# Kept turned blocks for the first SAGE pass of a two-layer graph network, its sixteen slots in a new order, two of six tests a graph in the gated part

## The chip, the cores and the metric

The kernel runs on one core of a Trainium2 chip, as one program. The metric is the device time of one execution in microseconds. Engines are named as the profile names them: PE is the matrix engine (PEld its weight loads), DVE the vector engine, ACT the scalar engine, POOL the GpSimd engine, and SP the engine that issues most DMAs here. Each engine runs its instructions in the order in which the program lists them, and waits on semaphores that other engines and landed DMAs raise.

## The reference, cut to what matters

There are 16 graphs of 1024 nodes and 128 channels, with a 0/1 adjacency. Layer 0 is a gated graph network of four steps on all graphs; layer 1 first thins the adjacency by a "skipping" that goes row by row, and then runs three SAGE layers with batch norm. Both layers are added to their input and normalised.

```python
def _gru_cell(m, h, ...):                       # layer 0, four times for each graph
    r, z, n = sigmoid(..), sigmoid(..), tanh(xn + r * hn)
    return (1.0 - z) * n + z * h

def step(carry, n):                             # layer 1: the skipping, row after row
    row = jnp.take(carry, n, axis=0)
    num, rank = jnp.sum(row), jnp.cumsum(row)
    sf = jnp.where(num > T_DIL, (num + K_DIL - 1) // K_DIL, 1)
    rm = row & (rank % sf == 0)
    carry = carry.at[n].set(row & ~rm)                 # removed from the row
    carry = carry.at[:, n].set(carry[:, n] & ~rm)      # and from the column

def _sage(x, adj, Wr, Wx, b, mf):               # three times, batch norm between
    deg = jnp.clip(jnp.sum(adj, axis=-1, keepdims=True), 1.0, None)
    out = (jnp.einsum('bij,bjd->bid', adj, x) / deg) @ Wr + x @ Wx + b
    return out / jnp.maximum(jnp.linalg.norm(out, axis=-1, keepdims=True), 1e-12) * mf[..., None]
```

## The kernel before, in words

The order of every engine's instructions is written out by hand: the program text is the order, and pools of rotating tiles decide only which buffer a tile gets, and with it what a refill has to wait for.

**The gated part** (classes `Gated` and `FixPoint`) takes the first 1280 us. Two graphs run through the four steps of layer 0 in turn (streams 0 and 1, `layer`), and between PE's matmuls `beside` puts the steps of the skipping, one piece at each of ten points `aside(0)` to `aside(9)` of a layer. The skipping works on blocks of 128 rows of four graphs at once. For block row k of a graph it needs what earlier block rows removed from its first k*128 columns: these are read back from DRAM (`not_r`), turned by a transposing DMA into a tile `f_rt` (`read_back`, `read_last`), and `keep` (L729) applies them. The signed result of each block row, which has -0.5 or 0.5 at an edge and 0 elsewhere, goes to `not_r` in DRAM in bf16 (`rows`, L867). Each pair of layers also tests one block of 128 rows of the adjacency for values other than 0 and 1 (`load_test`, `check`, `look` at L1982); two of the eight blocks of a graph are tested here.

**The first SAGE pass** (`Sage.first`) takes the next 470 us. The loop runs over b from -1 to 15, and each turn has sixteen slots, t = 0 to 15 (`slot`). A slot holds work on graph b (`now`) and work that prepares graph n = b + 1 (`nxt`):

- For graph n, sixteen *units* build the thinned adjacency turned, `p_at`, an fp32r tile. A unit turns four blocks of `not_r` on PE (p_u, L1482). Where a block lies above the diagonal, ACT makes it 0 or 1 with a Relu (L1487). Elsewhere DVE compares the block of `p_nr` in place with the turned block in PSUM (L1495, `unit_low`). POOL then *packs* each half row to bytes (`pack`, L1503, tile p_b), which go to DRAM in two halves for the later passes (L1689 and L1681, `s_at`).
- Graph n's input is normalised (L1517 to L1531), turned (L1418) and split into two parts, p_xh by ACT (L1412) and p_xl by POOL (L1413).
- For graph b, PE aggregates with 8 + 8 matmuls of 512 columns for each half (`agg`, L1564, p_xh then p_xl). ACT evicts each half to s_ag (`evict`, L1570; two buffers), writes the degree row in f16 (L1551), PE turns it to columns (L1557), DVE makes 1/degree from it (L1559, L1560). PE multiplies with the weights (`out_first`, L1579 to L1584), DVE scales (L1388, L1389), ACT squares (L1396, L1397), DVE makes the rows s_r (L1402 to L1407), and these are split again into p_rh (ACT) and p_rl (POOL).
- PE aggregates a second time with p_rh and p_rl, for the next SAGE layer. ACT evicts these two banks to s_ag at slot 15, and SP writes them to DRAM at slot 1 of the next turn (L1702).
- DVE tests the remaining six blocks of a graph, which SP loads (p_a, L1458, L1982).

The loop's work for graph 0 also holds `first_weights` (L1304 to L1310), which needs weights that `load_given` loads in the turn b = -1. `constants` stands ahead of the loop.

After it come the second and third pass and the head, which the change does not touch.

Of the kernel before, what the change touches and what calls it, by code (L numbers as in the profile page):

```python
# [21 lines left out]
P = 128  # L22
# [607 lines left out]

class FixPoint:
# [20 lines left out]
    def __init__(self, ctx, tc, cst, adj, not_r, bad):  # L652
        self.tc, self.nc, self.cst, self.adj, self.not_r, self.bad = tc, tc.nc, cst, adj, not_r, bad
        nc, G = self.nc, self.G
# [69 lines left out]

    def keep(self, i, g, a):
        k = self.todo[i][0]
        if k:
            rt = self.left.pop((i, g))
            self.nc.vector.scalar_tensor_tensor(a[:, :k * P], rt[:, :k * P], 0.0, a[:, :k * P],  # L729
                                                op0=ALU.is_ge, op1=ALU.mult)  # L730
# [9 lines left out]
    def steps(self):  # L740
# [5 lines left out]
        for i, (k, b0) in enumerate(self.todo):  # L746
# [41 lines left out]
            self.count(i, 1, a[1], rank, pt)  # L788
            if i == 0:

                for c in range(G, self.LOTS):
                    self.load(c)
# [125 lines left out]
class Gated:  # L918
# [72 lines left out]
    def load_test(self, n):  # L991
        if n < B * 2:
            self.test = self.wk.tile([P, N], F32, name="h_test", bufs=1)
            self.nc.sync.dma_start(self.test, self.adj[n // 2, n % 2 * P:(n % 2 + 1) * P, :])

    def check(self, n):
        junk = self.wk.tile([P, N], BF, name="h_junk", bufs=1)
        look(self.nc, junk, self.bad, self.test, n // 2, n % 2)
# [160 lines left out]
    def beside(self, st, ot, l, s, b0, steps):  # L1159
# [33 lines left out]
        def aside(n):  # L1193
# [8 lines left out]
            if n == 1 and s == 1 and not checked:  # L1202
                self.check(b0 // 2 * L0 + l)
                checked.append(l)
# [5 lines left out]
class Sage:  # L1210
# [14 lines left out]
    def __init__(self, ctx, tc, cst, adj, not_r, summed, nodemask, W, vec, Wl, bl, out, bad):  # L1225
        self.tc, self.nc, self.cst = tc, tc.nc, cst
# [29 lines left out]
    def load_given(self):  # L1256
# [10 lines left out]
        nc.sync.dma_start(self.vr[9:, :], row(bl))  # L1267
        self.m48 = self.wk.tile([P, NB, C], F32, name="p_rh", bufs=1).rearrange("p a b -> p (a b)")[:3 * B, :]
# [31 lines left out]
    def first_weights(self):  # L1300
# [9 lines left out]
        nc.vector.tensor_copy(self.mask48, self.m48)  # L1310
# [111 lines left out]
    def first(self):  # L1422

        nc, tc, cst = self.nc, self.tc, self.cst
        with ExitStack() as c:
# [17 lines left out]
            self.load_s(0)  # L1443
            self.eps = self.const([P, 1], 1e-5, "s_eps")
# [5 lines left out]
            self.constants()  # L1450
# [10 lines left out]
    def load_nr(self, b, f):  # L1461
        if b < B:
            g = self.g.setdefault(b, {})
            if f == 0:
                g["nr"] = self.nrp[b % 2].tile([P, NB, N], BF, name="p_nr")
            self.nc.sync.dma_start(g["nr"][:, 4 * f:4 * f + 4, :], rows_of(self.not_r[b, f * HF:(f + 1) * HF, :]))
# [7 lines left out]
    def unit(self, b, t):  # L1474

        nc, g, f, j = self.nc, self.g[b], t // 8, t % 8
        if t == 0:
            g["at"] = self.atp[b % 2].tile([P, NB, N], FR, name="p_at")
        v, at = g["nr"], g["at"]
        pu = self.ps2.tile([P, HF], F32, name="p_u")  # L1480
        for i in range(4):
            nc.tensor.matmul(pu[:, i * P:(i + 1) * P], v[:, 4 * f + i, j * P:(j + 1) * P], self.cst["ident_b"],  # L1482
                             start=True, stop=True)
        low = min(max(j + 1 - 4 * f, 0), 4) * P
        c0 = f * HF
        if low < HF:
            nc.scalar.activation(at[:, j, c0 + low:c0 + HF], pu[:, low:], AF.Relu, scale=2.0)  # L1487
        g["pu"] = pu, low

    def unit_low(self, b, t):  # L1490

        g, f, j = self.g[b], t // 8, t % 8
        (pu, low), c0, v = g.pop("pu"), f * HF, g["nr"]
        if low:
            self.nc.vector.scalar_tensor_tensor(g["at"][:, j, c0:c0 + low], v[:, j, c0:c0 + low], 0.0, pu[:, :low],  # L1495
                                                op0=ALU.is_lt, op1=ALU.is_lt)

    def pack(self, b, t):
# [4 lines left out]
        self.nc.gpsimd.tensor_copy(g["b", f][:, j, :], g["at"][:, j, f * HF:(f + 1) * HF].bitcast(F32))  # L1503
# [38 lines left out]
    def degrees(self, b, f):  # L1542
# [7 lines left out]
        nc.vector.tensor_scalar(g["rho"][:, cols], deg, 1.0, None, op0=ALU.min)  # L1550
        nc.scalar.copy(g["row"][:, cols], deg)  # L1551

# [9 lines left out]
    def agg(self, pa, hi, at, f, js, start, stop):  # L1562
        for n, j in enumerate(js):
            self.nc.tensor.matmul(pa, hi[:, j, :], at[:, j, f * HF:(f + 1) * HF],  # L1564
# [37 lines left out]

    def slot(self, b, t):

        nc, g, n = self.nc, self.g.get(b), b + 1
        now, nxt = b >= 0, n < B

        if nxt:
# [4 lines left out]
            if t in (10, 13):  # L1613
                self.load_a(n, 2 + t // 13)
        if now and t in (0, 2, 5, 8):
            self.load_a(b, (0, 2, 5, 8).index(t) + 4)

        if now:
            if t in (2, 5):
                g["ag", t // 5] = self.evict(g.pop(("pa", t // 5)), -1, 0)  # L1620
            if t == 15:
                g["ag2"] = [self.evict(g.pop(("pb", f)), b, f) for f in range(2)]
        if nxt:
            self.unit(n, t)
            if t != 6 or not now:
                self.unit_low(n, t)
            if t:
                self.pack(n, t - 1)
        if now and t == 0:
            self.pack(b, 15)  # L1630
        if now:
            bank = lambda: self.ps3.tile([C, HF], F32, name="p_ag")
            if t in (2, 5):
                self.degrees(b, t // 5)
            if t in (0, 1, 3, 4):
# [4 lines left out]
            if t in (5, 7):  # L1640
                self.out_first(b, t // 7)
            if t in (6, 8):
                f = t // 8
                g["o", f] = self.scale_rows(b, f, g.pop(("oa", f)), g.pop(("ob", f)))
                if t == 6 and nxt:
                    self.unit_low(n, t)
# [3 lines left out]
            if t in (7, 9):  # L1650
                f = t // 9
                g["r", f] = self.rows(b, f, g.pop(("o", f)), g.pop(("ss", f)))
            if t in (8, 10):
                self.split_r(b, t // 10)
            if t in (6, 8):
                g["ss", t // 8] = self.squares(g["o", t // 8])
            if t in (11, 13):
                self.turn_r(0, b, t // 13, self.ps1)
            if t in (9, 10, 12, 14):
                part = g["rl"] if t in (10, 14) else g["rh"]  # L1660
                js = range(4 * (t // 12), 4 * (t // 12) + 4)
                for f in range(2):
                    if t == 9:
                        g["pb", f] = bank()
                    self.agg(g["pb", f], part, g["at"], f, js, t == 9, t == 14)

        if nxt:
# [4 lines left out]
            if t in (6, 8):  # L1672
                self.turn_x(n, t // 8)
            if t in (7, 12):
                self.split_x(n, t // 12)
        if now and t in (2, 5, 8, 10, 12, 14):
            self.check(b, (2, 5, 8, 10, 12, 14).index(t) + 2)

        if now:
            if t == 2:  # L1680
# [4 lines left out]
            if t in (13, 15):  # L1685
                nc.sync.dma_start(self.rt[b, t // 15], g["rt", t // 15])
        if nxt:
            if t == 10:
                nc.sync.dma_start(self.at8[n, 0], self.g[n]["b", 0])  # L1689
            if t == 13:  # L1690
                nc.sync.dma_start(self.x1[n], self.g[n]["s"])
        if (b, t) == (-1, 11):
            self.load_given()
# [4 lines left out]
        if (b, t) == (0, 3):  # L1698
            self.first_weights()
# [316 lines left out]
def kernel(ctx: ExitStack, tc: tile.TileContext, x, adj, nodemask,  # L2016
# [7 lines left out]
    with ExitStack() as ctx:  # L2024
        dram = ctx.enter_context(tc.tile_pool(name="e_dram", bufs=1, space=DRAM))
        not_r = dram.tile([B, N, N], BF, name="e_nr")
        summed = [dram.tile([P, NB, C], F32, name=f"e_sum{b}") for b in range(B)]
        with ExitStack() as c:
            gru = Gated(c, tc, cst, x, adj, weight, w_ih, w_hh, b_ih, b_hh, summed, bad)
            fix = FixPoint(c, tc, cst, adj, not_r, bad)  # L2030
            c.enter_context(tc.manual_schedule(engines={ET.PE, ET.DVE, ET.Activation, ET.Pool, ET.SP}))
            gru.run(fix.steps())
        sage = Sage(ctx, tc, cst, adj, not_r, summed, nodemask, W, vec, Wl, bl, out, bad)
# [34 lines left out]
```

## Time and profile before

| what | time |
|---|---|
| median of 3 runs | 2207.2 us (2204.59 to 2207.37) |
| the profiled execution | 2207.94 us |
| its span, first to last instruction | 2206.2 us |
| PE busy | 2099.8 us, 95% |
| DVE busy | 1836.0 us, 83% |
| ACT busy | 1327.2 us, 60% |
| POOL busy | 1233.9 us, 56% |
| mean granted TensorE clock | 0.986 |

The profile's lines are read like this. A group of instructions has its line in the kernel, engine, operation, out<-in, and how often it ran; then busy time and mean duration; then how long the engine sat idle just before them, and who ended that. A row of the order of time gives start, duration, engine, line, operation, tiles, and in brackets the idle time before it with its releaser. A row of a stretch gives, for each engine, busy time and number of instructions, then the granted clock, the busy share of the 16 DMA engines and GB/s. A row of waits says who waited for whom, in total, how many times, and the longest.

### The profile page before, as it was taken

What the parts mean: (1) busy time and instruction counts of PE and PEld (TensorE: products, weight loads), DVE (VectorE), ACT (ScalarE), POOL (GpSimd) and SP (SyncE); (2) the same over time, 40 slices, a digit from 0 to 9 for tenths busy, and PEclk for the clock granted to TensorE, in tenths of its full rate; (3) what the DMA queues carried; (4) which work ended last, traced back from release to release, by engine and by line L of the source; (5) the groups of instructions that cost most, each with busy time, mean ns of one, the idle gap of its engine ahead of it and who ended that gap; (6) DMA issues with size and microseconds to landing.
All of it is one profiled execution on the core that took longest, in us unless ns stands there. A gap on an engine that the chain in (4) does not pass through costs nothing. (4 is left out here: it accounts for less than half of the span.)

```text
span 2206.2 us, 32924 instructions
## 1 busy us (share of the span) xinstructions
PE 2099.8 (95%) x10217; PEld 1441.5 (65%) x10217; DVE 1836.0 (83%) x4213; ACT 1327.2 (60%) x3238; POOL 1233.9 (56%) x1218
## 2 busy tenths in 40 slices
PE   6999999999999999999999979999999899999987
PEld 4666556666666665666655657777777678887865
DVE  4898998889998889989889978888888666766877
ACT  3657466565656666465575656666666355555756
POOL 4458558567476475585575457777777255540002
PEclk9999999999999999999999989999999999999989
DMA  8247446366364394472584178888887577764404
GB/s 254 76 107 244 90 115 223 85 179 184 84 202 129 80 256 110 91 241 78 126 237 101 52 263 309 304 306 306 305 305 259 210 249 248 248 225 171 139 30 143
DMA packets 233853, 406.13 MB, mean 184 GB/s; under 512 B 79042, under 2 KB 100196, under 8 KB 233668
## 3 DMA queue, kind: packets, MB, share of 16 engines
q1 hardware_dynamic: 187844, 284.37, 39.4%
q0 software_dynamic: 41472, 117.46, 19.8%
q10 hardware_dynamic: 4352, 2.11, 0.4%
q8 instruction: 83, 1.36, 0.2%
q14 instruction: 102, 0.84, 0.1%
HBM read 313.48 MB, written 109.25 MB: 192 GB/s over the span
## 5 line engine op out<-in xcount | busy, mean ns | idle before, releaser
L1104 PE MATMUL h_g<-h_h,h_wh 128*128 128x512 f32 x768 | 396.1, 597 | 3.3 <-DVE h_r L1116 3.3
L1104 PE MATMUL h_g<-h_ms,h_wi 128*128 128x512 f32 x768 | 392.2, 592 | 0.0
L1123 POOL TENSOR_TENSOR h_zh<-h_r,h_h 128x512 f32<-128x512 f32 x126 | 174.2, 1382 | 257.2 <-ACT h_r L1119 254.0
L737 DVE TENSOR_TENSOR_SCAN f_rank<-f_a,f_first,f_pd 128x1024 f16<-128x1024 bf16 x128 | 299.4, 2345 | 4.2
L1092 PE MATMUL h_g<-h_a,h_hi 128*128 128x512 f32 x1024 | 278.7, 413 | 1.0 <-DMA h_a<-in_adj_dram 0.9
L1503 POOL CAST p_b<-p_at 128x512 uint8<-128x512 f32 x256 | 219.8, 881 | 84.7 <-DVE p_at L1495 52.7
L1104 PEld LDWEIGHTS h_g<-h_ms,h_wi 128*128 128x128 f32 x768 | 145.5, 190 | 184.3 <-issue 168.9
L1092 PE MATMUL h_g<-h_a,h_lo 128*128 128x512 f32 x1024 | 261.8, 392 | 0.0
L1092 PEld LDWEIGHTS h_g<-h_a,h_hi 128*128 128x128 f32 x1024 | 190.1, 188 | 61.7 <-issue 22.2
L1396 ACT ACTIVATE s_junk<-s_o 128x128 bf16<-128x128 f32 x384 | 114.0, 298 | 175.2 <-DVE s_o L1389 164.6
L1092 PEld LDWEIGHTS h_g<-h_a,h_lo 128*128 128x128 f32 x1024 | 189.8, 188 | 38.6 <-DVE h_lo L1030 0.4
L1104 PEld LDWEIGHTS h_g<-h_h,h_wh 128*128 128x128 f32 x768 | 133.3, 190 | 100.3 <-issue 72.7
L1125 POOL TENSOR_TENSOR h_h<-h_h,h_zh 128x512 f32<-128x512 f32 x126 | 179.9, 1428 | 9.9
L1119 ACT ACTIVATE h_r<-h_r,h_bi 128x512 f32<-128x512 f32 x128 | 92.4, 722 | 149.2 <-DVE h_r L1118 149.2
L1124 POOL TENSOR_TENSOR h_zh<-h_z,h_zh 128x512 f32<-128x512 f32 x126 | 162.1, 1287 | 9.9
L1095 ACT COPY h_ms<-h_g 128x512 f32<-128x512 f32 x128 | 73.8, 577 | 150.8 <-PE h_g L1092 150.6
L910 ACT ACTIVATE f_u<-f_rank,f_q 128x128 f16<-128x128 f16 (+7 forms) x128 | 110.6, 867 | 70.2 <-DVE f_rank L850 70.2
L1771 PE MATMUL q_ob<-s_wxp,q_xt 128*128 128x256 f32 x512 | 125.7, 390 | 0.3
L1982 DVE SCALAR_TENSOR_TENSOR p_junk<-p_a 128x1024 bf16<-128x1024 f32 x96 | 125.7, 1309 | 0.0
L1495 DVE SCALAR_TENSOR_TENSOR p_at<-p_nr,p_u 128x128 fp32r<-128x128 bf16 (+1 forms) x192 | 102.5, 543 | 19.4 <-ACT p_at L1487 12.6
L887 ACT ACTIVATE f_pd<-f_rank,f_q 128x128 f32<-128x128 f16 x128 | 59.1, 462 | 96.5 <-DVE f_q L701 93.4
L1413 POOL TENSOR_TENSOR q_rl<-s_r,q_rh 128x512 fp32r<-128x512 f32 x32 | 41.2, 1288 | 128.8 <-ACT q_rh L1412 105.8
(256 smaller groups left out, 4770.7 us busy)
## 6 DMA issues: line engine op xcount, KB each, us to landing
h_a<-in_adj_dram POOLq DMA_DIRECT2D x128, 512.0 KB, 9.2
p_a<-in_adj_dram SPq DMA_DIRECT2D x96, 512.0 KB
f_a<-in_adj_dram POOLq DMA_DIRECT2D x128, 256.0 KB, 6.5
e_nr<-f_nr SPq DMA_DIRECT2D x128, 256.0 KB
p_nr<-e_nr SPq DMA_DIRECT2D x32, 1024.0 KB
h_test<-in_adj_dram SPq DMA_DIRECT2D x32, 512.0 KB
s_at<-p_b SPq DMA_DIRECT2D x32, 512.0 KB
s_ag<-s_ag SPq DMA_DIRECT2D x64, 256.0 KB
```

What stands on the lines that cost most here:

```text
L737: nc.vector.tensor_tensor_scan(out, a, other[:, 0, 0:1].to_broadcast([P, N]), start, op0=ALU.add, op1=ALU.bypass)
L910: nc.scalar.activation(u[:, :n1], rank[:, g, :n1], AF.Abs, bias=q[:, 1, g:g + 1], scale=q[:, 0, g:g + 1])
L1092: nc.tensor.matmul(pm[f], part[:, j, :], st.adj[j][:, half[f]], start=(j == 0 and n == 0), stop=(j == NB - 1 and n == 1))
L1104: nc.tensor.matmul(pg, lhs, rhs, start=(i == 0), stop=(i == len(mm) - 1))
L1123: aid.tensor_tensor(d, r, h, ALU.subtract)
L1124: aid.tensor_tensor(d, z, d, ALU.mult)
L1125: aid.tensor_tensor(h, h, d, ALU.add)
L1396: self.nc.scalar.activation(junk, o[:, i, :], AF.Square, accum_out=ss[:, i:i + 1])
L1495: self.nc.vector.scalar_tensor_tensor(g["at"][:, j, c0:c0 + low], v[:, j, c0:c0 + low], 0.0, pu[:, :low], op0=ALU.is_lt, op1=ALU.is_lt)
L1503: self.nc.gpsimd.tensor_copy(g["b", f][:, j, :], g["at"][:, j, f * HF:(f + 1) * HF].bitcast(F32))
L1771: nc.tensor.matmul(pb[:, i], g["xt"][:, f, blk], self.wxp, start=(i % 2 == 0), stop=False)
L1982: nc.vector.scalar_tensor_tensor(junk, a, 0.0, a, op0=ALU.is_gt, op1=ALU.not_equal, accum_out=bad[:, c:c + 1])
```

## The change

1. **Turned blocks are kept.** After block row k of the skipping has its `f_rt` tiles, `send` writes them to a new DRAM tensor `e_vt` (four DMAs on SP for each block row but the first of a graph: 112 in all). The first SAGE pass loads them back (`g["low"]`), and loads of `not_r` only the blocks on and below the diagonal, in eight DMAs of growing width; together they fill the same tile `p_nr`.
2. **Fewer transposes.** PE turns only the blocks on and above the diagonal, 36 of 64, in twelve units. The diagonal block is masked by DVE against PSUM (`unit_own`); all below it is masked by `unit_low` in one instruction for each block row, against the kept turned blocks, with both operands in SBUF. `p_at` becomes eight tiles.
3. **The sixteen slots are laid out anew**, by four tables (UNITS, LOWER, PACKS, TESTS) and moved conditions: output matmuls, scaling, squares, rows and splits one slot earlier or merged; the second degree columns behind the second output matmuls; packs of block rows 4 to 7 of the first half late; the write of the second byte half to slot 0, that of the first half to slot 14; evictions of the second aggregation to slot 14. `load_given` goes ahead of the loop, `constants` and `first_weights` into the turn b = -1, the load of the node mask and its copy on their own.
4. **Two of six tests a graph move** to the gated part, which now loads and tests two blocks in each pair of layers, at `aside(0)` and `aside(1)` of the second stream.

```diff
+    def send(self, i):
+        k, b0 = self.todo[i]
+        if k:
+            for g in range(self.G):
+                self.nc.sync.dma_start(self.turned[b0 + g, :, below(k) * P:below(k + 1) * P],
+                                       self.left[i, g][:, :k * P])
...
             self.count(i, 1, a[1], rank, pt)
+            self.send(i)
...
+        self.tests = []
+        for i in (2 * n, 2 * n + 1):
+            t = self.wk.tile([P, N], F32, name="h_test")
+            self.nc.sync.dma_start(t, self.adj[i // 4, i % 4 * P:(i % 4 + 1) * P, :])
...
-            if n == 1 and s == 1 and not checked:
-                self.check(b0 // 2 * L0 + l)
+            if n in (0, 1) and s == 1 and n not in checked:
+                self.check()
...
+            for k in range(4 * f, 4 * f + 4):
+                self.nc.sync.dma_start(g["v"][k], self.not_r[b, k * P:(k + 1) * P, :(k + 1) * P])
+                if k == 4:
+                    self.nc.sync.dma_start(g["low"], self.turn[b])
...
+    def mask(self, out, v, turned):
+        self.nc.vector.scalar_tensor_tensor(out, v, 0.0, turned, op0=ALU.is_lt, op1=ALU.is_lt)
+    def unit_own(self, b, j):
+        g, own = self.g[b], slice(j * P, (j + 1) * P)
+        self.mask(g["at"][j][:, own], g["v"][j][:, own], g.pop("pu"))
+    def unit_low(self, b, j):
+        g = self.g[b]
+        self.mask(g["at"][j][:, :j * P], g["v"][j][:, :j * P], g["vt"][j])
...
+    UNITS = {0: 0, 1: 1, 2: 2, 3: 3, 5: 8, 6: 9, 7: 10, 8: 11, 10: 12, 11: 13, 13: 14, 14: 15}
+    LOWER = {1: 1, 2: 2, 3: 3, 4: 4, 9: 5, 10: 6, 11: 7}
+    PACKS = {1: (0,), 2: (1,), 3: (2,), 4: (3,), 5: (4,), 6: (8,), 7: (9,), 8: (10,), 9: (11,),
+             10: (5,), 11: (6, 12), 12: (7, 13), 14: (14,), 15: (15,)}
+    TESTS = {2: 4, 5: 5, 7: 6, 12: 7}
...
-            if t == 15:
+            if t == 14:
                 g["ag2"] = [self.evict(g.pop(("pb", f)), b, f) for f in range(2)]
...
-            if t in (5, 7):
-                self.out_first(b, t // 7)
-            if t in (6, 8):
-                f = t // 8
+            if t in (4, 6):
+                self.out_first(b, t // 6)
...
+            if t in (5, 7):
+                f = t // 7
                 g["o", f] = self.scale_rows(b, f, g.pop(("oa", f)), g.pop(("ob", f)))
+                g["ss", f] = self.squares(g["o", f])
...
             if t in (3, 6):
                 pt = bank() if t == 6 else self.ps1.tile([P, 4, P], F32, name="s_tr").rearrange("p a b -> p (a b)")
                 self.degree_columns(b, t // 6, pt[:, :4])
-            if t in (7, 9):
-                f = t // 9
+            if t in (6, 8):
+                f = t // 8
                 g["r", f] = self.rows(b, f, g.pop(("o", f)), g.pop(("ss", f)))
+                self.split_r(b, f)
+            if t in (4, 6):
+                self.degree_row(b, t // 6)
...
-            if t == 2:
+            if t == 0:
                 nc.sync.dma_start(self.at8[b, 1], g["b", 1])
...
-            if t == 10:
+            if t == 14:
                 nc.sync.dma_start(self.at8[n, 0], self.g[n]["b", 0])
...
+        if (b, t) == (-1, 8):
+            self.constants()
+        if (b, t) == (-1, 9):
+            self.first_weights()
...
         if t == 1 and b >= 1:
             for f in range(2):
                 nc.sync.dma_start(self.ag[b - 1, f], self.g[b - 1]["ag2"][f])
```

## The prediction

> **What bounds the kernel now.** I read the busy times by stage first, then the wait list of the first SAGE pass, then its groups of instructions, and last one graph of it in order of time, engine by engine. The two stages that the change edits:
>
> ```profile
> core 0: us, PE busy (x) PEld busy (x) DVE busy (x) ACT busy (x) POOL busy (x), PEclk, DMA share, GB/s
> 600.00:1000.00 400.00, 396.41 (x1485) 241.21 (x1484) 353.79 (x723) 248.69 (x468) 259.96 (x256) 1.00 0.56 157
> 1350.00:1700.00 350.00, 332.48 (x2406) 265.21 (x2407) 307.36 (x783) 225.79 (x634) 255.07 (x254) 1.00 0.87 303
> ```
>
> The first row is the gated part: PE is idle 3.6 us of 400. The second is the pass: PE 95%, DVE 88%, POOL 73%, DMA engines 87%. Its graphs follow at 27.73 us (the first p_ag matmul of each graph stands at 1330.96, 1358.69, 1386.41 in the order of time), but 34.54 us lie between those of graphs 0 and 1. So PE sets the pace, with some 1.3 us a graph lost to two waits (p_ag on p_rh, p_ag on p_rl). Three waits matter later (engine, waited for, us in total, times, longest):
>
> ```profile
> ACT s_ag L1570 <- DMA s_ag<-s_ag: 8.4, 7, 4.7
> PEld p_ag L1564 <- POOL p_rl L1413: 14.9, 15, 1.0
> DVE f_tr L904 <- PE f_pd L902: 39.6, 33, 2.4
> ```
>
> The first two are of the pass, the third of 200 to 1263 us. The first says that an s_ag buffer is refilled only when its DMA to DRAM has landed. One graph border in order of time, POOL's and SP's rows, then ACT's:
>
> ```profile
> 1523.59 1.28 POOL L1413 TENSOR_TENSOR p_xl<-p_s,p_xh 128x508 fp32r<-128x508 f32 x1
> 1524.81 3.85 POOL L1503 CAST p_b<-p_at 128x512 uint8<-128x512 f32 x5
> ...
> 1525.10 1.24 SPq L1702 DMA_DIRECT2D s_ag<-s_ag  x2
> 1526.54 0.33 SPq L1458 DMA_DIRECT2D p_a<-in_adj_dram  x1
> 1528.13 0.32 SPq L1681 DMA_DIRECT2D s_at<-p_b  x1
> ...
> 1530.64 0.59 ACT L1570 COPY s_ag<-p_ag 128x512 f32<-128x512 f32 x1 [0.40 <-DMA s_ag<-s_ag]
> ```
>
> The reader is to see three things. s_ag leaves SP 3 us ahead of the s_at write, which waits for POOL's last packing. It takes 1530.6 - 1525.1 = 5.5 us to land, and ACT's next eviction waits 0.4 us for that already. And five packs that cost 0.57 us each elsewhere (seven took 3.96) take 3.85 instead of 2.83, because a test ran on DVE meanwhile. Another pack, at 1503.79, took 1.88 beside a test of 1.21.
>
> **The change part by part.**
>
> **PE.** 64 block transposes a graph become 36. Eight of them in a row pitch 0.43 us (1501.95 to 1502.38), so 28 x 0.055 = 1.5 us a graph goes, on the engine that sets the pace.
>
> **DVE.** Two tests go: 2 x (1.31 + 0.08) = 2.8 us a graph. The masking was 6 x 0.67 + 2 x (0.55 + 0.42 + 0.27) = 6.5 us. It becomes 8 own blocks at 0.27 and seven lower parts of 128 to 896 columns from two SBUF operands. The nearest row is L729 (0.35, 0.45, 0.57, 0.95, 0.83, 0.96, 1.10 us), so 2.2 + 5.2 = 7.4 us. Net -1.9 of 24.3: DVE has room.
>
> **DMA.** 3584 columns of the old 8192 come from the new e_vt, so the bytes of p_nr stay; nine issues replace two, 0.4 us each on an SP that mostly waits. Two loads of 512 KB a graph leave: 8 MB become 7.
>
> **POOL.** 16 packs, two xl, two rl remain. What changes is beside what they run. The old masking read one operand from PSUM; the new lower parts read two from SBUF, as L729 and the tests do. An L729 of 1.08 us stretched POOL's L1123 from 1.29 to 1.89 (609.97).
>
> The Trainium skill ("SBUF — State Buffer", Practical consequences) says that a DVE instruction with two SBUF inputs contends with a GpSimd instruction that reads SBUF, and that the later one blocks fully; an instruction with one SBUF input doesn't. This speaks against the change: by it the 5.2 us of lower parts lock POOL out where the old 4.0 + 2.5 us did not. The rows bear the direction out, but show 0.6 to 0.7 of such an overlap for L729, nearly all for a test; by full locking the sum below would be 0.8 us a graph longer.
>
> **The new order closes a loop.** By the instruction order of the changed program, three things stand together that stood apart.
> (a) On POOL, after the second rl come packs 11 and 5, xl, packs 6, 12, 7, 13, xl, 14, 15. Before, only packs 9 and 10 lay between rl and xl.
> (b) On SP, the write of the second byte half moves from slot 2 to slot 0, ahead of the two s_ag writes of slot 1. So s_ag now leaves behind POOL's pack 15; the two p_b writes, s_ag and all p_nr loads queue behind that wait. ACT's eviction of ag0, and behind it the f16 degree row, wait for s_ag's landing. On PE the degree columns wait for that row, and the first output matmuls stand behind them.
> (c) In slot 6 the second degree columns now follow the second output matmuls on PE, and DVE's rdeg stands ahead of rows for half 0, whose result feeds rh, rl, and so the rest.
>
> One turn, from pack 15 to the next graph's pack 15:
> - SP: s_at issue 0.38 and hand-over, 0.45
> - s_ag landing: 5.5 above with queues 87% full. From below, 2.7 (s_at, issued 1294.52, awaited until 1297.22, hardly loaded) less the 0.4 that s_at leaves earlier: 2.3. I take 3.5, nearer the low end since a longer graph thins the traffic
> - ACT: eviction to row, 1502.39 to 1503.67, 1.3; hand-over 0.1
> - PE from the first degree columns to the end of the second: 0.19, 2.36 (output), 1.93 (eight p_ag), 0.22, 0.49, 0.22, 2.36, 0.25 = 8.0
> - DVE: rdeg 0.4, rows 1.4 (1512.30 to 1513.67); rho row 0.35, scale 1.5 (1513.59 to 1515.07) = 3.65
> - ACT squares 1.5 (1515.10 to 1516.63); DVE rows, half 1: 1.4 free, 2.6 where POOL held it (1516.66 to 1519.22), 1.6 taken; ACT rh and hand-over 0.7
> - POOL: 1.29 + 2 x 1.28 + 8 x 0.57 = 8.4; held by the parts of 768 and 896 columns and test 7 (0.96 + 1.10 + 1.21 = 3.3): none to 3.3, 2.5 taken by the rows above
>
> Sum 0.45 + 3.5 + 1.4 + 8.0 + 3.65 + 1.5 + 1.6 + 0.7 + 8.4 + 2.5 = 31.7 us. The low ends give 27.8, the high ends (5.5; 2.6; 3.3) 35.5. PE alone would need 27.73 - 1.5 - 1.3 = 24.9, so the loop sets the pace: +4.0 a graph. The wait comes before ag0 of graphs 1 to 15: 15 x 4.0 = +60 us (low +1, high +117).
>
> The skill ("DMA: Bandwidth & Descriptors", Anatomy of one DMA) fits a DMA as 2.0 us plus its bytes at 436 GB/s, an estimate of 2.6 us for these 256 KB. No wait on s_ag here shows less than 5. By it the loop would be 30.8 us and the pass +46.
>
> **The gated part.** 32 more tests, 1.54 + 0.08 us each here (L1982: 49.3 us for 32), 51.8 us on DVE over the whole part, some 16 of them in each 400 us, where DVE has 46 idle. Each stands at the head of a layer of the second stream, ahead of f_tr (L904), queued with settle, f_w and the gates behind it; in that very place DVE waits 39.6 us in 33 times for PE, 1.4 to 1.8 us in five blocks of eight, 0.6 in the three with the widest keep. So 12 x 0.9 = 11 us can't hide; about half should reach PE: +5. Bounds: -1 (nothing shown goes) and +14. The 112 sends (14.7 MB) and 32 test loads cost nothing: SP waits 583 us for f_nr in that stretch and DMA is at 0.56. If that cover went, the read-backs behind them would be late and keep's wait for f_rt (5.0 us in 3) would grow, within the +14.
>
> **Graph 0 and the ends.** First weights and constants move into the warm-up, away from graph 0, whose 34.54 us hold 6.8 too many (DVE waited 2.84 for the mask, PE 1.3 and 0.4 around L1304). In return two more packs and the lower parts precede the second xl, about 2.5 us: -4 (-7 to +1). The tail, with one test after the last rows: -1 (-2 to +1).
>
> **Sum.** +60 + 5 - 4 - 1 = +60. The profiled execution took 2207.94 us (span 2206.2), 0.7 above the median 2207.2, so 2268 for it and 2267 for the median.
>
> **The rivals.**
> *PE keeps the pace* (faster). If pack 15 ended so early that s_ag lands within the 5 us between PE's last rl matmul and ag0's eviction, the pass would run at 24.9, or at 26.4 with the 1.5 us that point (c) puts before rh: 15 x -1.3 to -2.8 = -20 to -42, with the rest 2165 to 2188. For it: PE's row above, DVE's and DMA's loads fall. Against: after its last rl POOL still owes 7.1 us of its own, while PE's last rl matmuls take 1.9. It decides when pack 15 ends within 1 to 2 us of those matmuls (5.0 less 0.45 less a landing of 2.3 to 3.5).
> *The loop closes without s_ag* (about the same). With the landing hidden, POOL's chain to xl against PE's next p_xl gives 27 to 28 us a graph: -10 to +5, 2195 to 2214. For it: landings could shorten as DMA thins.
> *The gated part becomes DVE-bound on top*: all 51.8 us of tests reach PE; 2310 to 2320. Against: the L904 wait is there to be filled.
>
> **How the numbers follow.** Loop 0.74, PE pace 0.11, loop without s_ag 0.11, gated bound 0.04. The loop case alone: 2235 to 2300. All together, for 8 in 10, 2206 to 2302: it leaves out the PE case and the top. Faster by over 0.2% (4.4 us, about what this kernel's measurement can tell) 0.15: PE's case and a third of the third; the same 0.04; slower 0.81.
>
> **What would show it.** Right: the new eviction line of s_ag waits on its own DMA some 3 to 5 us in each graph; graphs 31 to 32 us apart; SP stands before the second p_b write; PE busy below 85% in the pass, its waits on degree rows; POOL's casts longer; L904's wait in the gated part nearly gone. Wrong: no wait of ACT for s_ag, graphs 25 to 26.5 us apart, or a gated part longer by over 15 us.

## The result, and the profile after

The changed kernel takes **2314.3 us** (median of 4 runs, 2303.97 to 2322.42) against 2205.9 us for the kernel before beside it: 1.049 times as long, 95% interval 1.045 to 1.053. The forecast was 2267, with a range of 2206 to 2302. The direction was right; the time lies 12 us above the range.

The profiled execution took 2322.42 us (span 2320.7, before 2206.2). Where the 114.5 us of span went, between marks that both traces have (the start of the last f_rank row of settle in the gated part, L850 before and L864 after; the first p_ag matmul of a graph in the pass; the end of the pass's last p_ag):

| stretch | before | after | difference | forecast |
|---|---|---|---|---|
| start to last settle (gated part) | 1259.1 | 1287.9 | +28.8 | +5 |
| last settle to the first p_ag of graph 0 (border) | 37.3 | 55.3 | +18.0 | in the -4 of "graph 0" |
| first p_ag of graph 0 to that of graph 15 | 423.9 | 481.0 | +57.1 | +60, and -4 for graph 0 |
| first to last p_ag of graph 15 (tail) | 26.3 | 34.9 | +8.6 | -1 |
| the rest | 459.5 | 461.6 | +2.1 | 0 |

One execution of each kernel was profiled, here the slowest of the four. How far such a mark can be trusted: in the seven kernels here that have this gated part the last settle lies between 1287.2 and 1291.2 us, and in five others that leave the pass as it is here the third row is 467 to 485 us.

The two stages of the forecast, in the changed kernel (busy time and instructions of each engine, granted clock, DMA share, GB/s):

```profile
600.00:1000.00 400.00, 390.12 (x1453) 236.90 (x1452) 367.55 (x746) 239.75 (x451) 259.40 (x248) 1.00 0.59 174
1350.00:1700.00 350.00, 292.29 (x1818) 232.87 (x1817) 262.70 (x676) 195.65 (x567) 209.62 (x221) 0.95 0.68 233
```

In the pass PE is busy 83.5% instead of 95%, every other engine has become idler too, and the DMA share falls from 0.87 to 0.68. That is a loop of waits, not a full engine. The clock fell from 1.00 to 0.95. The waits of the same stretch that reach PE, and two of 200 to 1288 us after them:

```profile
PE p_u L1508 <- DVE p_at L1518: 28.8, 11, 2.6
...
PE p_ag L1599 <- ACT p_rh L1431: 16.3, 18, 1.4
ACT s_ag L1605 <- DMA s_ag<-s_ag: 15.8, 11, 1.9
PE s_tr L1592 <- ACT p_rl L1582: 12.1, 11, 2.3
```

```profile
DVE f_tr L918 <- PE f_pd L916: 18.5, 12, 3.0
...
PEld h_g L1109 <- DMA h_a<-in_adj_dram: 10.5, 10, 1.7
```

One turn of the loop in order of time, PE first, then SP and ACT, then POOL and DVE:

```profile
1404.71 0.38 PE L1508 MATMUL p_u<-ident_b,p_nr 128*128 128x128 bf16 x4 [2.63 <-DVE p_at L1518]
1404.91 3.17 PE L1599 MATMUL p_ag<-p_at,p_xh 128*128 128x512 f32 x8
...
1413.13 0.25 PE L1592 MATMUL s_tr<-s_one,p_rl 1*128 1x1 f16 x4 [0.39 <-ACT p_rl L1582]
...
1420.93 0.25 PE L1592 MATMUL p_ag<-s_one,p_rl 1*128 1x1 f16 x4
...
1423.56 2.14 PE L1599 MATMUL p_ag<-p_at,p_rh 128*128 128x512 f32 x8 [1.39 <-ACT p_rh L1431]
```

```profile
1408.37 0.32 SPq L1722 DMA_DIRECT2D s_at<-p_b  x1
1408.78 1.22 SPq L1747 DMA_DIRECT2D s_ag<-s_ag  x2
...
1411.79 0.59 ACT L1605 COPY s_ag<-p_ag 128x512 f32<-128x512 f32 x1 [1.02 <-DMA s_ag<-s_ag]
...
1412.46 0.62 ACT L1582 CAST p_rl<-s_ag 1x512 f16<-1x512 f32 x1
```

```profile
1428.53 1.30 POOL L1432 TENSOR_TENSOR p_rl<-s_r,p_rh 128x512 fp32r<-128x512 f32 x1 [1.54 <-ACT p_rh L1431]
...
1432.54 2.28 DVE L2027 SCALAR_TENSOR_TENSOR p_junk<-p_a 128x1024 bf16<-128x1024 f32 x1
```

The reader can lay the forecast's loop on these rows. s_at leaves at 1408.37, s_ag at 1408.78 and lands 2.9 us later; ACT evicts at 1411.79, the row ends at 1413.08, PE's first degree columns start at 1413.13 and the second end at 1421.18; rows, squares and p_rh follow to 1428.45; POOL's second rl starts at 1428.53 and pack 15 ends some 10.8 us on, at 1439.3, 31 us after the one before. The steps measure 0.45 + 2.9 + 1.35 + 8.05 + 3.35 + 1.55 + 1.7 + 0.7 + 10.8 = 30.9 us; the forecast had 31.7. Beside it stands a wait that the forecast did not have: DVE runs the test of 2.28 us ahead of own blocks 6 and 7, and PE's next p_u waits 2.63 us for their bank. The lower parts of 768 and 896 columns and this test take 1.57, 1.25 and 2.28 us on DVE, beside POOL's packs and p_xl. The forecast had them at 0.96, 1.10 and 1.21 and let their meeting with POOL lengthen POOL's work alone.

At the border between the stages, the last writes of e_nr and the first load of p_nr, before and after:

```profile
1263.41 3.71 SPq L867 DMA_DIRECT2D e_nr<-f_nr  x4
1267.59 0.96 SPq L1466 DMA_DIRECT2D p_nr<-e_nr  x2
```

```profile
1291.58 4.19 SPq L881 DMA_DIRECT2D e_nr<-f_nr  x4
1314.71 2.24 SPq L1490 DMA_DIRECT2D p_nr<-e_nr  x5
```

Before, the load follows 0.5 us behind the writes; after, 19 us.

### The profile page after: what moved, and what is told of

It is laid out like the page before. It is cut to its first block, busy times and chain, and to the rows that moved or that the text cites. A ratio compares the mean times of both kernels' runs of the same rounds, so it can differ in the third digit from the quotient of the medians.

```text
span 2320.7 us, 32321 instructions
## 1 busy us (share of the span) xinstructions
PE 2116.7 (91%) x9769; PEld 1447.6 (62%) x9769; DVE 1881.4 (81%) x4261; ACT 1319.7 (57%) x3238; POOL 1246.1 (54%) x1218
## 5 line engine op out<-in xcount | busy, mean ns | idle before, releaser
L1535 POOL CAST p_b<-p_at 128x512 uint8<-128x512 f32 x256 | 212.7, 856 | 136.3 <-DVE p_at L1518 80.0
L1141 POOL TENSOR_TENSOR h_zh<-h_z,h_zh 128x512 f32<-128x512 f32 x126 | 190.7, 1513 | 9.9
L1508 PE MATMUL p_u<-ident_b,p_nr 128*128 128x128 bf16 x576 | 63.5, 231 | 59.6 <-DVE p_at L1518 50.4
L1054 PEld LDWEIGHTS h_g<-ident,h_h 128*128 128x128 f32 x512 | 62.7, 142 | 83.4 <-issue 75.8
L2027 DVE SCALAR_TENSOR_TENSOR h_junk<-h_test 128x1024 bf16<-128x1024 f32 x64 | 114.2, 1784 | 0.0
```

The source lines that it names most:

```text
L1141: aid.tensor_tensor(d, z, d, ALU.mult)
L1535: self.nc.gpsimd.tensor_copy(g["b", f][:, j, :], g["at"][j][:, f * HF:(f + 1) * HF].bitcast(F32))
L2027: nc.vector.scalar_tensor_tensor(junk, a, 0.0, a, op0=ALU.is_gt, op1=ALU.not_equal, accum_out=bad[:, c:c + 1])
```

## The experiments

Times are set against the changed kernel's 2314.3 and the kernel before's 2205 to 2208 us in the same sets of runs. "Last settle" is the mark of the table.

### The border

```diff
-            self.nrp = [pool(f"p_nr{i}", bufs=1) for i in range(2)]
             self.ap = pool("p_a", bufs=4)
+            self.nrp = [pool(f"p_nr{i}", bufs=1) for i in range(2)]
```

> The changed kernel with the pool of the tests (p_a) allocated ahead of the two p_nr pools, so that the first p_nr tile lies 16 KB further up, clear of the gated part's working pool, which the second h_test buffer has grown by 4 KB. Same instructions in the same order. Theory A (the first load of p_nr waits for the whole working pool of the gated part because their bytes overlap): its issue comes within 3 us of the last e_nr write instead of 19 us behind it, the first p_ag of graph 0 comes 13 to 19 us earlier, and the time falls by as much, to some 2296 to 2301 against 2314. Theory B (the load is late for another reason, such as a queue full of sends or the e_sum writes themselves): under 5 us.

Measured: 2293.3 us, ratio 1.039 (1.036 to 1.042). SP's rows at the border:

```profile
1292.63 3.76 SPq L881 DMA_DIRECT2D e_nr<-f_nr  x4
1298.20 2.24 SPq L1490 DMA_DIRECT2D p_nr<-e_nr  x5
```

The load now follows 1.8 us behind the writes, and from the last settle to the first p_ag it is 42.1 us instead of 55.3: 13.2 us come back, as theory A had it. The time fell by 21, more than theory A's 13 to 19; the rest lies in the pass and the tail, whose graphs vary with the clock (last section). In the changed kernel as built, the gated working pool ends at byte 164416 of a partition and the first p_nr begins at 162912, an overlap of 1.5 KB that came with the second 4 KB buffer for h_test (before, the pool ended at 160320). The load then waited for the last use of that pool: between 1285 and 1320 us SP's waits are 18.5 us for `e_sum<-h_x` in the changed kernel, and none for it in x_border. The overlapped bytes themselves belong to h_junk, not to h_x, so the wait is for the pool and not for these bytes alone. The last experiment shows the same wait from the other side. Some 5 us more than before remain at the border; they were not followed up.

### The gated part

```diff
 # g_onelook: the second test's look gives way to a one-column write of zeros
+        if i % 2 == 0:
             look(self.nc, junk, self.bad, t, i // 4, i % 4)
+        else:
+            c = tile_of(i // 4, i % 4)
+            self.nc.vector.tensor_scalar(self.bad[:, c:c + 1], t[:, :1], 0.0, None, op0=ALU.mult)
 # g_oneload: no second load and no second look; the one test runs at point 0
-        for i in (2 * n, 2 * n + 1):
+        for i in (2 * n,):
...
 # g_one_at1: as g_oneload, and the one test runs at point 1
-            if n in (0, 1) and s == 1 and n not in checked:
+            if n == 1 and s == 1 and n not in checked:
 # x_look12: both tests, at points 1 and 2
-            if n in (0, 1) and s == 1 and n not in checked:
+            if n in (1, 2) and s == 1 and n not in checked:
```

> The changed kernel with the second test of each pair of layers in the gated part left out; its block is still loaded, and DVE writes one column of zeros from it instead (so a value other than 0 and 1 in those blocks would go unseen). Theory A (the tests' time on DVE is what lengthened the gated part by 28 us): the last settle comes 14 to 25 us earlier. Theory B (the loads and sends on the DMA queues did it): under 6 us earlier. As forecast (5 us in all for the tests): 5 us.

> The changed kernel with the second test of each pair of layers in the gated part left out, load and look (those blocks are not tested at all; a zero is written in place of the result). If the 16 MB of loads delay the adjacency tiles h_a, whose waits on PE went from about 1 to 17 us, then the last settle comes a further 6 to 12 us earlier than with the look alone left out; if the loads cost nothing, as forecast, within 2 us of it; what then remains over the kernel before is the sends' part.

> The changed kernel with the two tests of the gated part at points 1 and 2 of the second stream's layer instead of points 0 and 1; as many tests as before. Theory P (what costs is the place: the test at point 0 stands ahead of f_tr and settle, ACT's f_u starts later by it, and DVE's f_w then waits for ACT, 2.5 us in a block instead of 0.7): the gated part gets shorter by 10 to 22 us. Theory D (DVE's time as such is what costs, wherever it stands): within 4 us of the changed kernel.

> The changed kernel with one test in each pair of layers of the gated part, as in the kernel before and at its point 1, and nothing at point 0 (the blocks of the second tests are neither loaded nor tested). So of the gated part only the sends and the second h_test buffer remain. Theory P (the place at point 0 costs most of the 28 us, since with one test at point 0 the last settle still came at 1281.9): the last settle comes at 1261 to 1265 us, and the place is worth 17 to 21 us, the second test itself 6. Theory Q (the place is worth only the 7.6 us by which the tests at points 1 and 2 were earlier, and sends beside loads the rest): 1270 to 1275.

g_send adds to the kernel before the function `send`, its call and the tensor e_vt, as in the diff of the change.

> The kernel before, with the 112 writes of turned blocks to e_vt added and nothing else changed (nobody reads them). As forecast: the sends cost nothing, within 3 us of the kernel before. Theory S (the sends are what is left of the gated part's 28 us after the tests are out): 15 to 22 us slower, with the last settle as much later.

| kernel | tests in a pair of layers | time, us | last settle, us |
|---|---|---|---|
| before | 1 at point 1 | 2205.9 | 1259.1 |
| before with sends (g_send) | 1 at point 1 | 2208.4, ratio 1.0008 (0.9996 to 1.0020) | 1261.8 |
| changed | 2 at points 0 and 1 | 2314.3 | 1287.9 |
| g_onelook | 1 at point 0, second one loaded | 2303.2 | 1285.4 |
| g_oneload | 1 at point 0 | 2299.8 | 1281.9 |
| g_one_at1 | 1 at point 1 | 2286.3 | 1260.5 |
| x_look12 | 2 at points 1 and 2 | 2304.7 (2290.6, 2318.7) | 1280.3 |

The sends cost at most a few us, as forecast. Taking the second look out gave 2.5 us and its load 3.5 more, little against the 4 us between kernels with the same gated part: theory A of the first run fell, and with a test at point 0 the second one's DVE time is not what lengthened this part. The place is: one and the same test costs 21.4 us more at point 0 than at point 1 (1281.9 against 1260.5), so theory P of the run g_one_at1 stands. DVE's wait for f_pd is 11.7 us in g_oneload, and in g_one_at1:

```profile
DVE f_tr L918 <- PE f_pd L916: 37.2, 32, 2.4
```

(200 to 1260 us.) The wait is back near the 39.6 us of before, while the changed kernel has 18.5. So 21 us of that wait were indeed filled, as the forecast said they would be, but the wait was no room. At point 0 the test stands ahead of f_tr and settle, and ACT's f_u waits for settle's f_rank. Those waits, before and after (the same stretches as above):

```profile
ACT f_u L910 <- DVE f_rank L850: 59.2, 28, 3.2
```

```profile
ACT f_u L924 <- DVE f_rank L864: 82.3, 27, 4.0
```

ACT's wait has grown by 23 us, about what DVE's has lost; in g_oneload it is 80.7 us, in g_one_at1 55.2, in x_look12 56.9. PE's own waits, from 200 us to the last settle, go the same way: for ACT's h_r 4.3 us before, 11.6 in the changed kernel, 12.9 in g_oneload and 4.4 in g_one_at1; for DVE's f_x, ahead of f_pd, 1.1, 5.0, 5.7 and 1.1. That h_r is late because f_u stands ahead of it on ACT is argued from the order of the program, not shown by itself. One test of the changed kernel, ahead of f_tr at 571.68, takes 2.02 us, where the waits filled were 1.2 us on the mean (39.6 in 33). At point 1 the test runs behind settle, while ACT makes f_u.

x_look12 splits the sum again: its gated part is 7.6 us shorter than the changed kernel's, less than theory P's 10 to 22 (its time, from two runs 28 us apart, says nothing). A second test at point 2 still costs 20 us over one test at point 1, so two tests a pair of layers were dear at both places tried. These 20 us hold the second load as well as the second look: the waits for h_a on PE and its weight loads are 17.5 us in x_look12, 16.7 in g_onelook, which keeps the load without the look, and 5.4 in g_one_at1. No run here takes the load alone off x_look12.

### The pass: two waits side by side

```diff
 # x_tests
-    TESTS = {2: 4, 5: 5, 7: 6, 12: 7}
+    TESTS = {2: (4,), 5: (5, 6), 7: (7,)}
 # x_agbuf
+            self.agp = pool("p_agp", bufs=4)
...
-        ... else self.wk.tile([C, HF], F32, name="s_ag")
+        ... else self.agp.tile([C, HF], F32, name="s_ag")
```

> The changed kernel with the test of block 6 moved from slot 7 to slot 5, and that of block 7 from slot 12 to slot 7; nothing else. Theory A (what holds the pass is DVE's row at the end of a graph: the test of 2.28 us stands ahead of the own blocks 6 and 7, and PE's next p_u waits 2.6 us for their bank): that wait goes, graphs follow at 28.5 to 30 us instead of 32.1, and the granted clock in the pass rises over 0.96; the time falls by 25 to 45 us. Theory B, as forecast (the loop runs over pack 15, the s_at write and the landing of s_ag): the packs come 1 us earlier and no more, so graphs stay over 31 us and the time falls by 0 to 15 us. Theory C (DVE has no room in slots 5 and 7): the waits on s_rdeg and p_rh grow and the time does not fall.

> The changed kernel with four s_ag buffers in a pool of their own behind all others, instead of two, in the first pass, so that no eviction waits for the landing of a write of the turn before. Theory B, as forecast (the loop runs over the landing of s_ag): ACT's wait for s_ag goes, and graphs come down from 32.1 us; but DVE's late own blocks hold the next border at 2.6 us after it, so by the trace of the changed kernel 1.0 to 2.5 us a graph, 15 to 38 us in all. Theory A (DVE's row alone sets the pace): ACT's wait goes and the time stays within 8 us.

> Both edits together: the tests of blocks 6 and 7 in slots 5 and 7, and four s_ag buffers. If the two waits stand in parallel (each alone is covered by the other, theory B with A behind it), the two together give far more than the sum of the edits alone (the tests alone gave 3.6 us): graphs of 27.5 to 29.5 us, a granted clock of 0.98 to 1.00 in the pass, 40 to 65 us less than the changed kernel, 2250 to 2275. If the loop closes over something else (POOL's packs to p_xl, the degree columns behind the second output matmuls), graphs stay over 30 us.

| kernel | time, us | ratio (interval) | mean graph, us |
|---|---|---|---|
| changed | 2314.3 | 1.049 (1.045 to 1.053) | 32.07 |
| x_tests | 2310.7 | 1.049 (1.046 to 1.052) | 31.68 |
| x_agbuf | 2287.0 | 1.036 (1.033 to 1.039) | 30.17 |
| x_tests_agbuf | 2255.1 | 1.021 (1.018 to 1.024) | 27.91 |

A mean graph is a fifteenth of the time between the first p_ag of graphs 0 and 15. The move of the tests alone, though PE stood 2.6 us a graph behind one of them, gave 3.6 us, less than either kernel's runs spread: theory A fell. In x_tests PE's wait at the border is down to 1.52 us, and more than the gain turns up behind s_ag, whose write leaves SP at 1569.99 (PE, then ACT):

```profile
1565.80 0.38 PE L1508 MATMUL p_u<-ident_b,p_nr 128*128 128x128 bf16 x4 [1.52 <-DVE p_at L1518]
...
1574.35 0.25 PE L1592 MATMUL s_tr<-s_one,p_rl 1*128 1x1 f16 x4 [2.11 <-ACT p_rl L1582]
```

```profile
1573.01 0.58 ACT L1605 COPY s_ag<-p_ag 128x512 f32<-128x512 f32 x1 [1.92 <-DMA s_ag<-s_ag]
```

The two waits cover one another: DVE's late own blocks hold PE while s_ag lands. The edits alone are worth 4 and 27 us, both together 59. That is the forecast's loop, with a second chain of nearly its length beside it. With the wait for s_ag gone and the border wait at 1.52 us the clock is whole again (x_tests_agbuf):

```profile
1350.00:1700.00 350.00, 311.09 (x2068) 249.35 (x2067) 296.35 (x762) 219.63 (x649) 223.05 (x246) 1.00 0.76 264
```

The clock has a part in the 59. In x_agbuf 13 of 14 border waits of 2.6 us were followed by half the clock, and these graphs, the last one aside, take 30.3 to 30.5 us; the one where the clock stayed at 1.00 takes 29.11. So of the 32 us between x_agbuf and both edits some 18 are the clock's (13 x 1.36) and some 15 the shorter border wait (14 x 1.1); this split is an estimate from these rows.

### What was left of the pass, and a faster version

All three build on x_tests_agbuf; x_rdeg puts the second degree columns ahead of the second output matmuls, x_turn moves the second turning of s_r behind units 14 and 15, x_all has x_turn, x_border and x_look12 together.

```diff
 # x_rdeg
+            if t == 6:
+                self.degree_columns(b, 1, bank()[:, :4])
             if t in (4, 6):
                 self.out_first(b, t // 6)
...
 # x_turn
-            if t in (10, 12):
-                self.turn_r(0, b, t // 12, self.ps1)
+            if t in (10, 15):
+                self.turn_r(0, b, t // 15, self.ps1)
...
```

> The changed kernel with the tests in slots 5 and 7, four s_ag buffers, and the second degree columns ahead of the second output matmuls on PE (point (c) of the forecast undone). If rdeg behind the output matmuls is what makes PE wait 1.4 us a graph for p_rh, then PE waits some 0.7 us for the degree row instead, graphs come at 27.2 to 27.5 us instead of 27.94, and the time falls 6 to 12 us below 2255. If the squares or ACT's row copy come last anyway, within 4 us, or slower.

Measured: 2243.6 us, most graphs at 27.50 us instead of 27.95. Point (c) of the forecast is worth 0.45 us a graph, 6.7 us; the rest of the 11.5 is not of the pass.

> The changed kernel with the tests in slots 5 and 7, four s_ag buffers, and the turning of the second half of s_r (four PE transposes, ACT's copy, DVE's statistics, the DMA of s_rt) moved from slot 12 to slot 15, behind units 14 and 15. What is left at the border is a round trip: PE's p_u waits 1.52 us for own block 6, which stands on DVE behind the statistics of s_rt, which wait for ACT's copy of PE's transposes. If that round trip is all, the wait goes, graphs follow at 26.2 to 26.8 us, below the 27.73 of the kernel before, and the time falls 17 to 26 us below 2255. If DVE or POOL now sets the pace, graphs stay over 27.3 us.

Measured: 2244.4 us, graphs at 27.33, a miss against 26.2 to 26.8. The wait for own block 6 fell from 1.52 to 0.2 us, but only 0.6 us a graph came of it: PE now waits for POOL's p_xl instead, as these rows of x_all show.

```profile
1463.09 1.21 PE L1600 MATMUL p_ag<-p_at,p_xl 128*128 128x512 f32 x4 [0.56 <-POOL p_xl L1432]
...
1476.74 2.11 PE L1600 MATMUL p_ag<-p_at,p_rh 128*128 128x512 f32 x8 [1.38 <-ACT p_rh L1431]
```

> All edits that took something away, together: tests in slots 5 and 7, four s_ag buffers, the second turning in slot 15, the pool of p_a ahead of the p_nr pools, and the gated part's tests at points 1 and 2. If each removes what it removed alone (13 us at the border, 7 us in the gated part, 59 us by the first two, and 17 to 26 us by the turning), the time is 2205 to 2220 us, level with the kernel before or up to 0.7% above it. If they cover one another, over 2225.

Measured: 2221.3 us, ratio 1.005 (1.004 to 1.007), 1 us above the expected range: the edits add, x_turn's shortfall aside.

The last pair mends both rows just shown: x_rdeg's edit, and the packs of block 7 behind POOL's second p_xl. x_fast4 leaves the two tests in the gated part; x_fast6 takes them back into the pass and the gated part back to one test at point 1 with one h_test buffer; it does without x_border's order of the pools.

```diff
...
-             10: (5,), 11: (6, 12), 12: (7, 13), 14: (14,), 15: (15,)}
+             10: (5,), 11: (6, 12), 13: (7, 13), 14: (14,), 15: (15,)}
 # x_fast6
-    TESTS = {2: 4, 5: 5, 7: 6, 12: 7}
+    TESTS = {2: (2,), 5: (3, 4), 7: (5,), 10: (6,), 14: (7,)}
...
```

> All five edits together, and two more in the pass: the second degree columns ahead of the second output matmuls, and the packs of blocks 7 (both halves) one slot later, behind POOL's second p_xl, for which PE waits 0.56 us a graph. Four tests a graph in the pass, two moved ones at points 1 and 2 of the gated part. If the waits go one by one, graphs come down from 27.33 to 26.2 to 26.9 us, and the time from 2221 to 2203 to 2215 us; the gated part stays 20 us longer than before. If DVE or POOL now sets the pace, graphs stay over 27.1 us and the time over 2216.

> The same pass, but with the two moved tests taken back: one test in each pair of layers of the gated part at point 1 with one h_test buffer, as in the kernel before, and six tests a graph in the pass (slots 2, 5, 5, 7, 10, 14). If the moved tests were a loss, the gated part comes back to 1260 to 1262 us at the last settle, the first load of p_nr comes early by itself, and the pass pays less than the 19 us gained: 2.6 us more of DVE a graph, of which 0 to 1 us reaches PE. Then 2190 to 2206 us, at or below the kernel before. If DVE has no room (graphs over 27.9 us), it is no faster than x_fast4.

Measured: x_fast4 **2201.2 us**, ratio 0.9977 (0.9968 to 0.9985), faster than the kernel before by 0.2% and 2 us below the expected range. x_fast6 2231.3, ratio 1.011 (1.010 to 1.013): its second case, that DVE has no room, came true. The pass of each (x_fast4, then x_fast6):

```profile
1350.00:1700.00 350.00, 334.26 (x2203) 265.42 (x2202) 307.52 (x828) 232.40 (x680) 253.41 (x273) 1.00 0.81 284
```

```profile
1400.00:1650.00 250.00, 223.33 (x1430) 175.84 (x1429) 230.20 (x573) 151.03 (x440) 178.23 (x176) 0.97 0.83 293
```

In x_fast4 PE is at 95.5% again and graphs follow at 26.04 us, so PE works 24.9 us a graph: the forecast's figure for PE alone. In x_fast6 DVE is at 92% and graphs take 28.6 us on the mean. Its gated part is 16.6 us shorter (last settle 1262.2 against 1278.8), but its pass is 36 us longer. Its border takes 55.3 us again, though it has only one h_test buffer: moving s_ag out of the pool below has put the first p_nr 4 KB lower (byte 158816), under the gated pool's end (160320). So the overlap is the cause, not the second buffer as such. Even without the 12.5 us by which this border is longer than x_fast4's, the two tests are dearer in the pass, at the slots tried, than in the gated part.

## Why the prediction was right and wrong

**Right in size, and in part by its mechanism: the pass.** "+4.0 a graph" measured +4.34 on the mean of all fifteen turns but graph 0's ((481.0 - 30.8) / 14 = 32.16, less (423.9 - 34.5) / 14 = 27.81), and graph 0's own interval fell by 3.8, so +60 - 4 stands against +57.1. The loop is there: its terms measured 2.9 us for the s_ag landing (3.5 taken), 3.35 for DVE's rows (3.65), 8.05 for PE's stretch (8.0), 10.8 for POOL with what held it (8.4 + 2.5). But it does not set the pace alone. Taking the landing out (x_agbuf) gave 27 us of the 57, because DVE's late own blocks hold PE as long; the forecast had "DVE has room" from the sum of DVE's work and gave no price to where its parts and tests stand at the end of a graph. The sign that was to show the loop was mis-sized: ACT waits for s_ag 0.9 to 1.9 us, not 3 to 5; PE's new wait at the border already delays the eviction. PE waited on the degree rows, as said, but only 12.1 us in eleven turns, and 28.8 us on the own blocks. POOL's casts did not get longer, 856 ns on the mean against 881. PE busy under 85% and graphs 31 to 32 us apart came true. The Trainium skill ("DMA: Bandwidth & Descriptors", Anatomy of one DMA) gave an estimate of 2.6 us for the landing, from a fit on GpSimd's path; the 2.9 us here, on SP's, stand nearer to it than the 3.5 of the forecast.

**That the size fits so well is luck.** The sum worked with a clock of 1.00; over the pass it measured 0.93. In the turns in which the clock fell at the border alone, PE's wait for the degree row is shorter instead (0.39 us in place of 2.00), and most of these graphs follow at about 30.95 us, 3.14 more than before: 14 x 3.14 = 44 us. With 3.8 off for graph 0, some 17 of the 57.1 us are left, most of them in six graphs of 32.5 to 34.1 us, in which the clock was at half on the loop itself (last section). So the loop was over-sized by 0.8 us a graph and the clock, which the forecast did not have, made it up. PE was busy 3.8 us more than before although some 23 us of transposes are gone (15 x 1.5), so the lower clock added some 26 us to its busy time; not all of that lengthened the pass.

**Wrong: "about half should reach PE: +5", bounds -1 and +14, for the gated part.** It measured +28.8, and with the next item it is what carried the time above the range. The step that failed is the one from DVE's wait in front of f_tr to room for a test: filled, yes, but at the cost of settle and of ACT's f_u behind it. g_one_at1 puts 21.4 us on the place of one test. "The sends cost nothing" held within the measurement; "test loads cost nothing" did not quite: 3.5 us, with 17 us of waits for h_a on PE and its weight loads instead of 4.

**Wrong: "graph 0 and the ends, -4 (-7 to +1)".** The step that failed is that the warm-up was costed by its instructions only. Graph 0's interval did fall by 3.8, but the border ahead of it grew by 18.0. The first load of p_nr waits for the pool of the stage before, which the second h_test buffer brought over p_nr's first bytes: 13.2 of the 18.0 us, by x_border.

**Wrong: "the tail, -1".** It is 8.6 us longer. The loop runs in graph 15 too, with no work of a next graph for PE to fill it: PE waits there 3.1 us for POOL's second p_xl, 2.8 for the degree row and 2.4 for p_rh. In x_fast4 the tail takes 24.9 us, 1.4 less than before.

**The rivals.** "The gated part becomes DVE-bound" named 2310 to 2320 and hit the time, but not by its mechanism: 28.8 us of the 51.8 reached PE, 21.4 of them by the place of one test, and the border and the tail gave the rest. "PE keeps the pace" is what the change can give once its waits are gone: x_fast4, with seven more edits, has a pass 31 us shorter than the pass before.

## What to carry to other kernels

A wait of an engine is room only if what stands behind it is not awaited by another engine: before an instruction is put into it, follow the row after the wait to the next engine. Where two chains of waits have nearly one length, mending either alone shows little; mend both in one run before calling either harmless. A buffer added in one stage can bring its pool over memory that the next stage loads first: compare that first load with the last use of the pool that lies there.

## What the runs showed of the hardware

The granted clock fell behind some of PE's short waits and not behind others. In a later graph of the changed kernel (order of time on PE, then stretches of it):

```profile
1758.75 0.38 PE L1508 MATMUL p_u<-ident_b,p_nr 128*128 128x128 bf16 x4 [2.63 <-DVE p_at L1518]
1758.95 2.08 PE L1599 MATMUL p_ag<-p_at,p_xh 128*128 128x512 f32 x8
...
1767.19 0.25 PE L1592 MATMUL s_tr<-s_one,p_rl 1*128 1x1 f16 x4 [2.00 <-ACT p_rl L1582]
1767.36 2.08 PE L1614 MATMUL p_oa<-s_wr,s_ag 128*128 128x128 f32 x8
...
1775.67 1.11 PE L1614 MATMUL p_oa<-s_wr,s_ag 128*128 128x128 f32 x8
```

```profile
1765.20:1767.10 1.90, 0.00 (x0) 0.00 (x0) 0.46 (x2) 1.26 (x4) 0.00 (x0) 1.00 1.03 287
1767.10:1774.80 7.70, 7.61 (x33) 6.36 (x34) 6.13 (x13) 3.12 (x9) 2.83 (x3) 0.56 1.00 353
```

After the idle 1.9 us the clock stood at 0.56 for the next 7.7 us (at 0.50 from 1767.4 to 1774.2), and the same eight matmuls took 2.08 us there and 1.11 us afterwards. In graphs of 31 us it fell behind the 2.63 us border wait instead, where eight p_xh matmuls took 3.17 us, not 2.08 as here. Which wait it is decides whether a turn of the loop takes 31 or 34 us: from the first degree columns to the end of the second, PE's stretch of the loop, it is 8.05 us in the first kind and 11.2 in this one (1767.19 to 1778.38).

These traces give no length of wait that decides. Of the changed kernel's 14 border waits of 2.6 us 8 were followed by half the clock and 6, like the one above, were not. In x_tests_agbuf no wait of 1.52 or 1.39 us was, but in x_fast6 5 of the 14 border waits of 1.4 us were, one of them at 1461.67, 2 us behind a wait of 0.49 (the eight p_xh after it took 3.32 us). The Trainium skill ("TensorE: Matmul & The Clock Gate", What's actually happening) gives half the clock after an idle window of some 3.4 us, free-running. The halving agrees; idle times of 1.4 to 2.6 us were enough here, though not each time.
